# Handing out the operations around each passage between attention and gated units in listed orders

## The chip, the cores and the metric

The kernel runs on one core of a Trainium2 chip. The metric is the device time of one execution in microseconds (us); lower is better. A core has five engines with one in-order queue each: TensorE (PE, matrix products and transposes), VectorE (DVE), ScalarE (ACT), GpSimd (POOL) and SyncE (SP), which issues most transfers. An instruction starts when it is first in its queue and the semaphores it waits for have come. Matrix products write to PSUM banks; other engines read them from there and so give the banks back.

## The reference

The input is (2, 2048, 256) in float32. A first attention block (compressed, selected and windowed attention, combined by gates) comes first, each part wrapped in a layernorm and a residual. Then come two layers of local attention and gated units, and these are where the change lies:

```python
def _layer(x, wqkv, qs, ksc, wo, lg, lb, w1, b1, w2, b2):
    h = shift_token(x)              # second half of the channels moved on by one token
    q, k, v = jnp.split(h @ wqkv, 3, axis=-1)        # 8 heads of 64
    q = l2norm(q) * qs
    k = l2norm(k) * ksc
    q, k = rotary_xpos(q, k)
    o = local_attention(q, k, v)    # windows of 128, each sees itself and the one before
    x = x + o @ wo
    h = shift_token(x)
    h = (h - mu) / jnp.sqrt(var + 1e-05) * lg + lb
    a, g = jnp.split(h @ w1 + b1, 2, axis=-1)        # 682 each
    return x + (a * jax.nn.gelu(g, approximate=False)) @ w2 + b2
for l in range(2):
    x = _layer(x, ...)
```

## The kernel before

The first attention block is recorded and then given out in a listed order (`FIRST`, `Notes.give_out`); it is the same in both kernels. The two layers of attention and gated units follow. There each operation is put into a list `todo` with a place, a number that stands for nanoseconds on a planned time line; at the end the list is sorted by place and every operation is issued in that order. Since each engine has its own in-order queue, the sorted list fixes the order on every engine.

Attention of a layer works on 32 tiles of 128 tokens (`ORDER`: 16 positions, the two batches alternating), one each 12400. For a tile `n` the operations are, with their engines:

- `turn_input` (PE transposes), `early_half`, `late_half` (ACT copies), `edge` (POOL): the shifted input `h`
- `project` j = 1, 0, 2 for keys, queries and values (PE, into a `pa` bank); `square` (ACT), `times` (DVE, rotary products, frees the bank), `values` (ACT)
- `sums`, `clip` (DVE), `power` (POOL), `add` and `unit` (POOL): the normed, rotated queries and keys; `table` (POOL) and `table_load` (SP) prepare the rotary tables
- `turn` (PE), `keys`, `queries` (ACT copies); `scores` (PE, two `pc` banks for each half of the heads), `tops` (DVE maxima with the mask, which frees these banks), `exps` (ACT), `divide` (DVE)
- `turn_probs` (PE, `pb` banks), `probs` (ACT copies), `weigh` (PE), `sum_first` (ACT) and `sum_both` (DVE), both into `oT`; `project_out` (PE) and `residual` (DVE)

The gated units work on eight groups of four tiles (`GORDER`: groups 0, 4, 1, 5, 2, 6, 3, 7), six chunks each, a chunk every 5170 (`STEP`). For a group `g`:

- `shift`: SP copies `Y[g]` one token on into `sh` with two transfers, one of them over 127 partitions, and for all but the first group of a batch a third one from `kept`; POOL writes a memset and `kept`. `sh` takes one of the two buffers that attention's `oT` uses.
- `moments` 0 to 3 (DVE statistics that read `sh`), `deviations` (POOL), `normed` (DVE), `turned` (PE transposes into a `pc` bank, evacuated by DVE), `second_bias` (POOL)
- `inner` (PE, w1), `gate` (ACT Gelu into `ge`, then DVE into `u`), `back` and `back_rest` (PE, w2), `back_add` (DVE)

In the planned order all `gate` operations stand behind the last `exps` (`max(place, no_gate_until)`), `shift` stands two chunks ahead of its `moments`, and the fetches of the next layer's weights have places of their own: `wqkv` and `wo` at 60000 behind the start of the last tile. A fetch that waits holds up what SP issues behind it: `wo` waits until the last `project_out` of the layer has read the old weights.

Banks of PSUM: two `pa`, two `pb`, four `pc`. In the profile nearly every instruction of the two layers has line 124, where `Engine.op` passes a call on; operations are told apart by the names of their tiles.

Of the kernel before, what the change touches and what calls it, by code (L numbers as in the profile page):

```python
# [74 lines left out]
983 870 990 963 904 931 967 965 966 932 968 969 933 970 934 937 935 984 994 971 991 995 936 992 938 972 993 976  # L75
939 997 973 996 940 998 999 977 1000 974 941 1001 975 943 978 942 1002 979 908 1006 871 1003 1007 980 873 905
1004 872 1008 981 909 1005 982 1009 910 911 1010 912 1011 1012
"""


# [73 lines left out]
def sandwich_kernel(ctx: ExitStack, tc: tile.TileContext, x, Wq, bq, Wk, bk, Wv, bv, Wo, bo, Wg, bg,  # L154
# [759 lines left out]
    todo = []  # L914

    def put(place, f, *args):
        todo.append((place, len(todo), f, args))
# [8 lines left out]
    TILE = 12400  # L926
# [265 lines left out]
    STEP = 5170  # L1192
# [154 lines left out]
    W[0]["wqkv"], W[0]["qks"] = attn_w  # L1347
    put(12000, fetch, 0, "wo")
    put(60000, fetch, 0, "gated")
    begin = 0  # L1350
    for l in range(DEPTH):
        last_tile = begin + (len(ORDER) - 1) * TILE
        attention(l, begin)
        units = last_tile + 28150
        last_chunk = units + (NCH * B * NG - 1) * STEP

        gated_units(l, units, last_tile + 37400, last_chunk + (-20000 if l + 1 < DEPTH else STEP))
        if l + 1 < DEPTH:
            put(last_tile + 60000, fetch, l + 1, "wqkv")
            put(last_tile + 60001, fetch, l + 1, "wo")  # L1360
            put(last_chunk + (GT + 1) * STEP, fetch, l + 1, "gated")
            begin = last_chunk - 20000
    with tc.manual_schedule():
        for place, _, f, args in sorted(todo, key=lambda x: x[:2]):
            f(*args)
# [47 lines left out]
```

## Time and profile before

| | us |
|---|---|
| three runs | 1602.71, 1603.73, 1606.21 |
| median | 1603.73 |
| profiled execution, its own time | 1604.54 |
| span of the profiled execution, first to last instruction | 1602.8 |
| first attention block and start (up to about 250) | 250 |
| attention of layer 0 to the gated units' steady state | 250 to 708 |
| gated units of layer 0 | 708 to 895 |
| attention of layer 1 with both passages | 895 to 1381 |
| gated units of layer 1 | 1381 to 1603 |

The span in 40 equal slices, each digit the busy tenths of a slice, and the tenths of full clock that TensorE was granted:

```profile
PE   7999967999999999799999989999999986999998
DVE  6588685787888888444444257888888884355553
ACT  5236554677677676311111146777776763111110
POOL 7205256766666666211111156666666661033243
PEclk9999989999999999889999999999999998999999
```

Slices 17 and 18 and slices 33 and 34 (counted from 1) are the passages into the gated units, slice 24 the one back. Inside attention and inside the gated units TensorE is busy all the time.

### The profile page before, as it was taken

The numbers are of one execution on the slowest core, as the hardware profiler recorded it, in microseconds if no ns is written. First come the engines' busy times: TensorE is split into PE (matmuls) and PEld (weight loads), VectorE is DVE, ScalarE is ACT, GpSimd is POOL, SyncE is SP. The second block draws the span as 40 slices with busy tenths as digits, with TensorE's granted clock in tenths as the row PEclk, the third lists the DMA queues.
The fourth block names the chain that finished last, engine by engine and source line by source line (L and its number), as shares of the span: only waits on it lengthen the run. The fifth ranks groups of instructions, "written<-read, shape, count | busy, mean of one in ns | idle before, by whom it ended". The sixth has DMA issues, their size and how long they took to land.

```text
span 1602.8 us, 32502 instructions
## 1 busy us (share of the span) xinstructions
PE 1519.0 (95%) x12344; PEld 993.6 (62%) x12344; DVE 1070.5 (67%) x3139; ACT 761.7 (48%) x2213; POOL 735.4 (46%) x906
## 2 busy tenths in 40 slices
PE   7999967999999999799999989999999986999998
PEld 6867743666666666455555556667666664555554
DVE  6588685787888888444444257888888884355553
ACT  5236554677677676311111146777776763111110
POOL 7205256766666666211111156666666661033243
PEclk9999989999999999889999999999999998999999
DMA  6000001100000000020000010000000000001000
GB/s 221 1 1 8 1 17 36 33 8 6 8 5 9 5 9 4 8 69 8 12 18 0 1 59 10 9 4 9 6 7 8 8 4 10 10 24 31 25 24 30
DMA packets 32510, 30.76 MB, mean 19 GB/s; under 512 B 5154, under 2 KB 30692, under 8 KB 32356
## 3 DMA queue, kind: packets, MB, share of 16 engines
q1 hardware_dynamic: 32164, 28.17, 5.8%
q8 instruction: 98, 1.61, 0.4%
q0 software_dynamic: 192, 0.52, 0.2%
q14 instruction: 56, 0.46, 0.1%
HBM read 20.30 MB, written 4.19 MB: 15 GB/s over the span
## 4 chain that ended last, share of the span: by engine, by line
PE 74%; DVE 4%; DMA 2%; POOL 1%; ACT 1%; issue 1%; POOLq 0%; SPq 0%; DVEq 0%; ACTq 0%
PE pa L124 29%; PE pb L124 23%; PE pc L124 22%; DMA sh<-Y 2%; DVE prob L124 2%; DVE rr L124 1%; POOL rr L124 1%; DVE Y L124 1%; ACT prob L124 0%; POOL ss L124 0%; DVE hh L124 0%; DVE st L124 0%; DVE ss L124 0%; ACT L124 0%; ACT ge L124 0%
## 5 line engine op out<-in xcount | busy, mean ns | idle before, releaser
L124 PE MATMUL pa<-wqkv,h 128*128 128x512 f32 x768 | 372.6, 608 | 15.1 <-ACT h L124 11.6
L124 POOL TENSOR_TENSOR rr<-rr 128x256 f32<-128x256 f32 x256 | 179.5, 733 | 311.3 <-DVE rr L124 259.3
L124 ACT ACTIVATE ge<-pa,vb 128x512 f32<-128x512 f32 (+1 forms) x107 | 67.0, 628 | 356.5 <-PE pa L124 320.9
L124 ACT ACTIVATE prob<-prob,off 128x192 f32<-128x192 f32 (+2 forms) x512 | 226.2, 445 | 12.7 <-DVE off L124 12.0
L124 PEld LDWEIGHTS pa<-wqkv,h 128*128 128x128 f32 x768 | 132.2, 192 | 128.4 <-issue 106.5
L124 ACT COPY probT<-pb 128x384 f32<-128x384 f32 (+1 forms) x256 | 119.9, 469 | 143.7 <-PE pb L124 140.7
L124 POOL TENSOR_TENSOR ss<-ss,mhalf 128x16 f32<-128x16 f32 x64 | 188.0, 2937 | 0.1
L124 PE MATMUL pa<-hh,w 128*128 128x512 f32 x368 | 176.2, 608 | 5.3 <-ACT ge L124 5.3
L124 DVE SCALAR_TENSOR_TENSOR u<-pb,vb,ge 128x512 f32<-128x512 f32 x73 | 54.8, 751 | 179.8 <-PE pb L124 179.4
L124 DVE CUSTOM_DVE_ANT_0 prob<-pc,mask_loc 128x192 f32<-128x192 f32 (+2 forms) x512 | 148.7, 346 | 28.8 <-PE pc L124 27.5
L124 PE MATMUL pc<-w,u 128*128 128x256 f32 (+1 forms) x896 | 165.3, 383 | 0.0
L124 PEld LDWEIGHTS pc<-w,u 128*128 128x128 f32 (+1 forms) x896 | 129.3, 173 | 50.6 <-issue 35.7
L124 DVE TENSOR_TENSOR rr<-pa,cs 128x1024 f32<-128x1024 f32 x128 | 150.7, 1216 | 10.8 <-ACT sq L124 10.8
L124 PE MATMUL pb<-hh,w 128*128 128x512 f32 x292 | 138.6, 597 | 0.0
L124 POOL TENSOR_TENSOR rr<-rr,ss 128x512 f32<-128x512 f32 x128 | 132.9, 1058 | 2.4
L124 DVE TENSOR_TENSOR prob<-prob,den 128x768 f32<-128x768 f32 x128 | 128.5, 1004 | 4.9
L124 PEld LDWEIGHTS pb<-ident,prob 128*128 128x128 f32 x752 | 89.8, 142 | 66.1 <-DVE prob L124 27.3
L124 PE MATMUL pb<-ident,prob 128*128 128x128 f32 x752 | 118.9, 280 | 11.4 <-DVE prob L124 9.6
L124 PE MATMUL pb<-wo,oT 128*128 128x256 f32 x512 | 123.2, 384 | 5.7 <-DVE oT L124 5.7
L124 POOL TENSOR_SCALAR r<-mv 128x1 f32<-128x1 f32 (+1 forms) x48 | 9.2, 193 | 247.8 <-DVE mv L124 245.4
L124 ACT ACTIVATE sq<-pa 128x512 f32<-128x512 f32 x128 | 75.9, 593 | 96.6 <-PE pa L124 93.8
L124 PE MATMUL pc<-kr,qT 64*64 64x192 f32 (+2 forms) x2688 | 111.0, 289 | 4.5 <-ACT qT L124 4.5
(255 smaller groups left out, 2500.8 us busy)
## 6 DMA issues: line engine op xcount, KB each, us to landing
cs<-in_rope_dram SPq DMA_DIRECT2D x32, 128.0 KB
out_dram<-res SPq DMA_DIRECT2D x32, 128.0 KB
sh<-Y SPq DMA_DIRECT2D x16, 254.0 KB
w<-in_L_ffn_w_dram SPq DMA_DIRECT2D x6, 640.0 KB
X<-_attn_hidden_states_dram SPq DMA_DIRECT2D x7, 512.0 KB
wqkv<-in_L_ffn_wqkv_dram SPq DMA_DIRECT2D x2, 1536.0 KB
Wc<-in_L_attn_Wc_dram SPq DMA_DIRECT2D x1, 1024.0 KB
wo<-in_L_ffn_wo_dram SPq DMA_DIRECT2D x2, 512.0 KB
```

The costliest lines, as they stand in the source:

```text
L124: return f(*a, **k)
```

## The change

The places stay as they are, and so do all operations. After the list is complete, three stretches of it are taken out: around the passage from attention into the gated units in each layer (300 operations, from two and a half tiles before the start of the last tile to nine chunks after the start of the gated units; the same list `TO_GATED` for both layers), and around the passage from layer 0's gated units into layer 1's attention (203 operations, `TO_ATTENTION`). In each stretch the operations, fetches of weights excepted, are given the sorted places again in the listed order: the operation with number `order[k]` gets the k-th place. Fetches keep their places, and so stand at the same rank among other operations than before. The lists were searched offline over a model of in-order queues; the model is not part of the kernel.

```diff
+TO_GATED = """
+39 42 140 0 1 21 26 3 25 28 2 89 9 22 11 17 31 37 19 24 5 8 58 18 20 34 7 12 15 29 41 47 14 4 45 60 27 6 36 48
...
+TO_ATTENTION = """
+45 47 125 128 78 5 18 9 25 10 12 2 6 8 26 33 28 16 17 11 13 30 38 14 37 36 39 7 63 67 19 29 42 43 23 52 70 15 75
...
-    begin = 0
+    begin, seams = 0, []
     for l in range(DEPTH):
         last_tile = begin + (len(ORDER) - 1) * TILE
...
         gated_units(l, units, last_tile + 37400, last_chunk + (-20000 if l + 1 < DEPTH else STEP))
+        seams.append((last_tile - 2.5 * TILE, units + 9 * STEP, TO_GATED))
         if l + 1 < DEPTH:
+            seams.append((last_chunk - 5 * STEP, last_chunk - 20000 + 5 * TILE, TO_ATTENTION))
...
+    def in_order(lo, hi, order):
+
+        part = sorted((x for x in todo if lo <= x[0] < hi and x[2] is not fetch), key=lambda x: x[:2])
+        order = [int(i) for i in order.split()]
+        assert sorted(order) == list(range(len(part)))
+        for x in part:
+            todo.remove(x)
+        todo.extend(part[k][:2] + part[i][2:] for k, i in enumerate(order))
+
+
+    for lo, hi, order in seams:
+        in_order(lo, hi, order)
```

Around the first three groups' `shift` and the first chunks the new order of `TO_GATED` reads, layer 0, with the rank in the stretch (`l0n29` is tile 29 of layer 0, `l0g4` group 4; the bank kinds stand behind `inner`):

```
 100 unit l0n29 0            206 inner l0g0 0 pa pc      281 sum_both l0n31
 101 turn l0n29 0            207 gate l0g0 0             282 project_out l0n31
 102 queries l0n29           208 queries l0n31           283 back l0g0 2
 103 shift l0g0              209 scores l0n31 1          284 residual l0n31
 104 moments l0g0 0          210 scores l0n31 0          285 back l0g0 1
 105 moments l0g0 2          ...                         286 gate l0g4 2
 106 moments l0g0 1          218 inner l0g0 5 pa pb      287 fetch 1 wqkv
 107 moments l0g0 3          219 gate l0g0 5             288 fetch 1 wo
 108 deviations l0g0         220 shift l0g4              289 shift l0g1
 109 exps l0n28 3            221 moments l0g4 0          290 moments l0g1 0
```

In the order before, the ranks are `shift l0g0` 49 and its first `moments` 88; `shift l0g4` 178 and 210; `shift l0g1` 265 and 279, ahead of both fetches (287, 288); the first `gate` 245, the last `exps` 244.

The gelu and the exp are in different function tables of ACT, which it loads with an instruction of its own.

## The prediction

> **What bounds the kernel now.** I read the page's busy shares first, then the stretches, then TensorE (PE) in order of time. PE is busy 95% of the span, so the time is PE's work plus what PE loses. The three stretches below are the three passages that the change touches; the columns are wall time, then busy PE, PEld, DVE, ACT, POOL, then granted clock, DMA share, GB/s.
>
> ```profile
> PE 1519.0 (95%) x12344; PEld 993.6 (62%) x12344; DVE 1070.5 (67%) x3139; ACT 761.7 (48%) x2213; POOL 735.4 (46%) x906
> 636.77:708.17 71.40, 55.33 (x435) 34.51 (x434) 34.45 (x97) 23.95 (x67) 15.81 (x14) 0.86 0.13 40
> 894.94:963.00 68.06, 62.52 (x330) 36.38 (x327) 29.93 (x73) 24.26 (x72) 31.07 (x42) 0.97 0.13 38
> 1312.18:1381.02 68.84, 51.94 (x435) 32.16 (x434) 34.51 (x97) 23.94 (x67) 15.81 (x14) 0.90 0.04 9
> ```
>
> First and third are attention into gated units (layers 0 and 1), the second is the way back. PE idles 16.1, 5.5 and 16.9 us there and then runs at half clock for a while. In full-clock steps of the PE timeline (1.72 us for four 128x512 matmuls, 1.75 for eight `wo`, 1.46 for a `weigh`, 0.8 for a `scores`, 0.49 and 0.35 for four and three transposes) a passage into gated units holds 14x1.72 + 4x1.75 + 3x1.46 + 3x0.8 + 6x0.49 + 11x0.35 = 44.7 us. So layer 0 loses 71.4 - 44.7 = 26.7 us, layer 1 68.8 - 44.7 = 24.1; the way back loses 5.5 idle and 3.3 us at half clock, 7.2. These 58.0 us are all that any order can win.
>
> The chain of waits, the DMA issues (SPq is SyncE's queue) and ACT show two things that an order must respect:
>
> ```profile
> 640.80 0.05 issue
> 640.85 0.20 POOL sh L124
> ...
> 641.65 16.04 DMA sh<-Y
> ...
> 1317.05 16.04 DMA sh<-Y
> ```
> ```profile
> 702.78 0.38 SPq L124 DMA_DIRECT2D wo<-in_L_ffn_wo_dram  x1
> 703.27 0.55 SPq L124 DMA_DIRECT2D sh<-kept  x1
> 703.88 1.46 SPq L124 DMA_DIRECT2D sh<-Y  x2
> ...
> 719.00:720.00 1.00, 1.00 (x5) 0.69 (x4) 0.37 (x1) 0.00 (x0) 0.00 (x0) 1.00 0.08 19
> 720.00:721.00 1.00, 1.00 (x6) 0.89 (x5) 1.00 (x4) 0.00 (x0) 0.29 (x1) 1.00 0.01 2
> ```
> ```profile
> 676.63 0.19 ACT L124 ACTIVATION_READ_ACCUMULATOR prob<-prob,off 128x1 f32 x1
> 676.82 1.28 ACT L124 ACT_TABLE_LOAD   x1
> 678.12 1.27 ACT L124 ACTIVATE ge<-pa,vb 128x512 f32<-128x512 f32 x2
> ```
>
> The transfer of `shift` (`sh<-Y`, 254 KB) lands 16.8 us after its issue (640.86 to 657.70), at 19 GB/s, in both layers; behind the `wo` load it ends 17.6 us after the matmul at 702.6 that let `wo` go. And ACT pays 1.28 us whenever it goes from exp to Gelu.
>
> **The change, part by part.** No instruction's shape changes; only queue positions do. I follow the changed order queue by queue, each operation priced by its row: `times` 1.13, `tops` 1.25, `divide` 1.0, a `moments` 0.64, `normed` 0.26, `u` 0.75 (DVE); Gelu 0.69, copy 0.47 to 0.59 (ACT); `power` 2.94, `unit` 1.06, deviations 1.2 (POOL). Before, `moments` stands far behind its `shift` (first group: issue 589.8, use 618.2). In the new order every moved `shift` is followed at once by its `moments`, on DVE, where all later work queues behind the wait. `shift` moves later past POOL's `add` and `unit`; its own memset and `kept` (0.2 and 0.3) hide there, and POOL has 54% free. SyncE needs only the `sh` buffer.
>
> A, first group, both layers. The buffer comes free with `project_out` of tile 26 (call its end 0), so the data lands at 16.9. DVE still has `residual` and two `tops` and stands at `moments` from 4.6. PE has a `turn`, two `scores`, three `turn_probs`, `turn_input`, two `project`, `weigh`, two `turn` and another `turn_input`, 0.5 + 1.6 + 1.05 + 0.2 + 3.4 + 1.5 + 1.0 + 0.2 = 9.5, and 1.7 in which it waits for ACT's copies of keys and inputs: 11.2 us. Then project 2 of tile 30 needs a `pa` bank that `times` frees, behind `moments`: 16.9 + 2.4 + 1.13 = 20.5. PE idles 20.5 - 11.2 = 9.3 us, twice. Second group: the buffer is free early enough that data and DVE arrive together (39.4 and 39.3 us on the same count): 0, and up to 7 if POOL's place set the issue, which the trace denies (issue 589.8, memset 606.6).
>
> B, table loads and banks, both layers. Gelu now stands among the exps: seven table loads per passage for one, 12 more in all, 12x1.28 = 15.4 us of ACT, of which PE feels what stands in front of it. Running the queues on from A: `queries` of tile 31 behind a Gelu with its load, 1.28 + 0.69 + 0.6 = 2.6 us; `inner` 1 wants a `pc` bank held by the last `scores` until Gelu, `u` and `tops` of the chunk before, 0.69 + 0.75 + 1.25 less a `turn_probs` = 2.5; `weigh` of tile 30 behind four exps and two loads, 1.0; a `turn_probs` behind `u` and `divide`, 1.9; `back` behind two evacuations and the last `u`, 1.8. Sum 9.8. It is soft: none of it if ACT (48% busy) runs ahead, twice it if each load is felt; I take 9.8, since the loads stand directly before what PE waits for.
>
> C, third group (`l0g1`). In layer 0 the fetches of `wqkv` and `wo` keep their places while `shift` moves behind them on SyncE's queue, so it is issued only when `wo` goes, after tile 31's `project_out`: exactly the three DMA rows above, 17.6 us. Then 2.4 for `moments`, 1.2, six `normed` 1.6, `u` 0.75, `back_add` 0.35: 23.9. PE has two `back`, one `inner`, one `back` and its rest, 2.2 + 3.4 + 1.1 + 0.6 = 7.3, then transposes that need `normed`. Idle 16.6 us. In layer 1 no fetch stands there; the issue comes after tile 30's `project_out`, 12.1 us of PE work earlier (three `inner` and a `project_out`), and idle is 16.6 - 12.1 = 4.5, less 0.5 without `wo`'s data in front: 4.0, bounds 0 and 7. The fourth group's transfer queues behind the third's: 0 to 2, taken as 0.
>
> D, the way back has no `shift`, no extra table load and the same fetches. The new order puts `project`, `inner` and `back` between transposes and `scores`, which covers the 2.25 us wait at 923.8 and the 0.5 to 0.7 us ones; remaining 2 us of 7.2, bounds 0 and 7.2.
>
> Clock. The rows show PE at 0.50 for 3.3 us after a wait of 2.2 us or more (659.9 to 663.0, 680.4 to 683.7), 1.65 us lost, 3.4 where a second wait follows. Four such waits per passage: 6.6 each. The Trainium skill (TensorE: Matmul & The Clock Gate, part 1) gives the window as 3.4 us and free-running, which these rows agree with; by its word that one idle window is needed, the two waits of 2.5 us in B might cost nothing, 3.3 us less per passage.
>
> Sum: layer 0 loses 9.3 + 9.8 + 16.6 + 6.6 = 42.3, layer 1 9.3 + 9.8 + 4.0 + 6.6 = 29.7, the way back 2: 74.0 for 58.0, +16. The profiled execution took 1604.5 us (span 1602.8 and 1.7 around it), the median of the runs is 1603.7: 1603.7 + 16 = 1620.
>
> One rule speaks against the order outright: the Trainium skill (DMA: Bandwidth & Descriptors, "Rules for kernel authors") says to issue early and wait late. The same page ("Why a DMA increments its semaphore by 16 and not by 1") says that a transfer over 127 partitions uses one DMA engine; the rows' 0.08 share, 1.3 of 16 engines, agrees. From its 27 GiB/s per engine and 2 us fixed, an estimate of the landing is 11 us instead of 16.8; by it A would be 3.5 us, C 10.8 and 0, and the time 1598. The trace's 16.8 decides.
> On table loads the skill (ScalarE: Activation LUTs, "What ACT_TABLE_LOAD costs") adds 1.38 us of drain to each; the rows above show none (load ends 678.10, Gelu starts 678.12). With it ACT would lose 16.6 us more.
>
> **Rivals.**
> Faster: the queues run ahead and B vanishes, the layer-1 transfer of C is covered and the way back is clean. For it: DVE, ACT and POOL have 33 to 54% free. Losses 9.3 + 16.6 + 3.3 and 9.3 + 1.7, 40.2 in all, 1604 - 18 = 1586. It decides once B is under some 5 us a passage. Against: the loads are in the order, and ACT is one queue.
> About even: A and C as I have them, B halved with two restarts fewer per passage: 16 - 9.8 - 6.6 = -0.4, 1603.
> Much slower: every table load is felt and restarts cost 3.4 each: B 19.6 per passage, so 2x9.8 + 8x1.75 = 33.6 on my sum, 1654; half of that, 1637, is as far as I go.
> That the change does nothing is out: the orders differ on all five queues in the three passages.
>
> **Numbers.** Forecast (A and C stand, B between half and one and a half times) 0.66; much slower 0.12; about even 0.08; faster 0.14. This kernel's measurement can tell 0.2%, 3.2 us. Of the forecast's 0.66 nearly all lies over 1606.9: slower 0.79, same 0.07, faster 0.14. Time 1620; range 1600 to 1637, from just below even to half of the worst B.
>
> **What would show it.** In the new profile: the chain of waits passes through `DMA sh<-Y` at three places in layer 0; DVE's wait for `DMA sh<-Y` rises from 2.0 us to some 35 in sum over both layers; PE has a wait near 9 us before a `wqkv` matmul in each layer and one near 16 before the transposes of `hh` in layer 0; 15 table loads instead of 3; the way back at full clock. I am wrong if `shift` lands well under 16 us after its issue, or if DVE comes to `moments` late.

## The result and the profile after

The changed kernel takes 1628.09 us (median of four runs, 1626.39 to 1628.78) against 1604.20 before (1602.71 to 1606.21): a ratio of 1.0146, 95% interval 1.0134 to 1.0158. The profiled execution took 1627.85 us with a span of 1626.1, so 23.3 us of span were added to 1602.8.

The page of the changed kernel: busy time, share and number of instructions of an engine, then the tenths of the clock that TensorE was granted, then the chain that ended last.

```profile
PE 1518.6 (93%) x12344; PEld 989.9 (61%) x12344; DVE 1064.0 (65%) x3139; ACT 773.9 (48%) x2225; POOL 736.3 (45%) x906
PEclk9999979999999998998999999999999989999999
PE 70%; DVE 4%; DMA 4%; ACT 3%; POOL 2%; issue 1%; SPq 0%; POOLq 0%; DVEq 0%; ACTq 0%
```

PE's busy time is that of before (1519.0) to 0.4 us, although the span is 23.3 us longer. So PE was given no more work; it waits longer. ACT has 12 instructions more (2213 before), the table loads, and 12.2 us more (761.7 before).

What PE waits for, and what DVE waits for (sum, number of waits, longest):

```profile
PE pa L147 <- DVE rr L147: 19.3, 5, 9.2
PE pc L147 <- DVE Y L147: 15.4, 3, 13.9
PE pb L147 <- DVE prob L147: 11.8, 6, 2.8
...
PE pb L147 <- ACT probT L147: 7.3, 6, 3.1
PE pc L147 <- ACT probT L147: 5.7, 4, 2.6
```
```profile
DVE st L147 <- DMA sh<-Y: 42.7, 6, 16.8
```

Before, DVE waited 2.0 us in sum for `sh<-Y`, now 42.7. The two largest waits of PE are for DVE: DVE is the one that stands still, and PE only inherits it. The same in order of time on PE in layer 0; in brackets stands the idle time ahead of the instruction and who ended it.

```profile
635.82 3.78 PE L147 MATMUL pa<-wqkv,h 128*128 128x512 f32 x4 [9.17 <-DVE rr L147]
...
648.45 0.84 PE L147 MATMUL pb<-ident,prob 128*128 128x128 f32 x6 [2.64 <-DVE prob L147]
...
678.62 0.55 PE L147 MATMUL pb<-ident,prob 128*128 128x128 f32 x3 [3.10 <-ACT probT L147]
...
693.59 0.56 PE L147 MATMUL pc<-probT,v 64*64 64x128 f32 x16 [2.63 <-ACT probT L147]
...
697.46 1.54 PE L147 MATMUL pb<-ident,prob 128*128 128x128 f32 x6 [2.80 <-DVE prob L147]
...
722.65 4.48 PE L147 MATMUL pc<-w,u 128*128 128x256 f32 x20
...
730.40 3.35 PE L147 MATMUL pc<-w,u 128*128 128x256 f32 x26
747.62 1.12 PE L147 MATMUL pc<-ident,hh 128*128 128x128 f32 x4 [13.87 <-DVE Y L147]
```

The chain of waits names what stands behind the first and the last of these:

```profile
616.15 16.12 DMA sh<-Y
635.82 3.78 PE pa L147 x4
...
724.74 16.20 DMA sh<-Y
748.74 3.41 PE pa L147 x4
```

In layer 1 the same five waits of the first group and of the exponentials are there (9.01, 2.60, 3.09, 2.63 and 2.77 us), and the last one is 1.30 us, where layer 0 has 13.87.

Where the 23.3 us came from is read off one event that both traces have, POOL's copy `kept` of a group. The eighth `kept` (the last group of layer 0) starts at 829.73 before and at 851.36 after, 21.6 later, of which 0.7 us was there before the change begins (POOL's `power` at 589.62 before stands at 590.27 after). The last one of all starts at 1507.63 and 1530.96, 23.3 later. In between, the way back takes 61.06 us where it took 68.06 (894.94 to 963.00 before):

```profile
916.58:977.64 61.06, 59.89 (x322) 33.56 (x321) 32.18 (x81) 25.49 (x74) 31.87 (x38) 1.00 0.14 43
```

So layer 0's passage costs 21.0 us more, the way back wins 7.0, and layer 1's passage costs 8.7 more: +0.7 + 21.0 - 7.0 + 8.7 = +23.4 (23.3 before rounding). The offset wanders by some 0.3 us inside layer 1's attention, so the parts are known no better than that.

### The profile page after: what moved, and what is told of

The parts are those of the page before. It is cut to its first block, busy times and chain, and to the rows that moved or that the text cites. A ratio compares the mean times of both kernels' runs of the same rounds, so it can differ in the third digit from the quotient of the medians.

```text
span 1626.1 us, 32484 instructions
## 1 busy us (share of the span) xinstructions
PE 1518.6 (93%) x12344; PEld 989.9 (61%) x12344; DVE 1064.0 (65%) x3139; ACT 773.9 (48%) x2225; POOL 736.3 (45%) x906
## 4 chain that ended last, share of the span: by engine, by line
PE 70%; DVE 4%; DMA 4%; ACT 3%; POOL 2%; issue 1%; SPq 0%; POOLq 0%; DVEq 0%; ACTq 0%
PE pa L147 27%; PE pb L147 23%; PE pc L147 20%; DMA sh<-Y 4%; ACT L147 1%; DVE hh L147 1%; DVE prob L147 1%; POOL rr L147 1%; ACT prob L147 1%; DVE rr L147 1%; DVE u L147 1%; POOL ss L147 1%; DVE Y L147 1%; ACT ge L147 0%; DVE st L147 0%
## 5 line engine op out<-in xcount | busy, mean ns | idle before, releaser
L147 PE MATMUL pb<-ident,prob 128*128 128x128 f32 x752 | 118.3, 280 | 18.5 <-DVE prob L147 11.8
L147 DVE TENSOR_TENSOR prob<-prob,den 128x768 f32<-128x768 f32 x128 | 124.9, 976 | 4.9
```

The source lines that it names most:

```text
L147: return f(*a, **k)
```

## The experiments

All are built on the changed kernel unless it says before. Each batch of runs has its own runs of the kernel before beside it (median 1603.92 to 1604.97).

| run | what is different | us | ratio to before, 95% |
|---|---|---|---|
| changed kernel | | 1628.09 | 1.0146 (1.0134 to 1.0158) |
| back_only | only the list of the way back | 1597.74 | 0.9958 (0.9941 to 0.9975) |
| third_first | `shift l0g1` ahead of the fetches | 1614.36 | 1.0062 (1.0045 to 1.0079) |
| wait_later | first group's `moments` later on DVE | 1615.87 | 1.0066 (1.0046 to 1.0087) |
| split | transfer cut into 112 + 15 partitions | 1589.94 | 0.9902 (0.9886 to 0.9919) |
| split_prime | transfer cut into 113 + 14 partitions | 1623.07 | 1.0120 (1.0103 to 1.0137) |
| grouped | 3 table loads per passage in place of 7 | 1611.03 | 1.0041 (1.0027 to 1.0056) |
| split_grouped | both | 1570.88 | 0.9791 (0.9775 to 0.9808) |
| split_identity | split, Gelu replaced by the identity: no table loads in the layers | 1568.63 | 0.9779 (0.9763 to 0.9795) |
| before_split | before, with the transfer cut | 1600.47 | 0.9969 (0.9956 to 0.9982) |
| back_split | back_only, with the transfer cut | 1590.71 | 0.9915 (0.9898 to 0.9931) |

**The way back alone.**

```diff
-    for lo, hi, order in seams:
+    for lo, hi, order in seams[1:2]:
```

> Only the list for the way back is given out; both passages into the gated units keep the order before. My account: the changed kernel's offsets say that this list saves 7.0 us, so 1597 (1595 to 1599) against 1604. Rival, that the way back gained only because the passage in front of it came out differently: 1604, as before.

Measured: 1597.74 us. From 1604.94 beside it that is -7.2 us, what the trace of the changed kernel gives for the way back inside the whole (-7.0). So the way back's gain does not hang on the passages, and the two passages into the gated units cost 1628.1 - 1597.7 = 30.4 us.

**The third group's shift ahead of the fetches** (265 is `shift l0g1`, 247 `project_out` of tile 30; both layers):

```diff
+        if order[0] == 39:
+            order.remove(265)
+            order.insert(order.index(247) + 1, 265)
```

> The changed kernel, with shift of the third group given out right behind tile 30's project_out, ahead of the fetches of wqkv and wo. My account (step C: the transfer queues behind wo, which waits for the last project_out): the 13.9 us wait of PE in layer 0 shrinks to some 1.5 us, the restart goes with it, 1628 - 12.5 - 2 = 1613 (1611 to 1616); layer 1 unchanged. Rival, that DVE is late there for its own work: 1628.

Measured: 1614.36 us, 13.7 less. In order of time on PE, the wait before the transposes of `hh`:

```profile
735.86 0.66 PE L147 MATMUL pc<-ident,hh 128*128 128x128 f32 x4 [2.14 <-DVE Y L147]
```

13.87 us have become 2.14. Of the 13.7 us, 11.7 are this wait; what is left of the gain fits the half clock that followed it (0.55 from 748 to 753 in the changed kernel, 2.3 us lost). So it was the place behind the fetches on SP's queue that made layer 0's third group late.

**The first group's statistics later on DVE** (88 and 95 to 110 are the four `moments` and the `deviations` of `l0g0`, 143 is its first `normed`):

```diff
+        if order[0] == 39:
+            late = [order.pop(order.index(88)) for _ in range(1)] + [order.pop(order.index(i)) for i in (100, 95, 105, 110)]
+            order[order.index(143) : order.index(143)] = late
```

> The changed kernel, with the first group's four moments given out behind times, sum_both and sums of the next tile, shift where it is. My account (step A: what is queued behind the wait on DVE costs, not the transfer itself): the 9.2 and 9.0 us waits of PE before project 2 of tile 30 go, at most 2 us of each come back, 1628 - 16 - 3 = 1609 (1606 to 1615). Rival, that the wait only moves to the next bank on the path: 1625 or more.

Measured: 1615.87 us, 12.2 less, and just outside of what was expected. PE's wait of 9.17 us is gone, but in its place stands, a little later:

```profile
638.58 1.51 PE L147 MATMUL pb<-ident,prob 128*128 128x128 f32 x6 [5.87 <-DVE prob L147]
```

DVE still comes to the `moments` before the data, but now by 2.04 us instead of 10.01, and what queues behind them is a `divide` instead of a `times`. Ahead of that `divide` DVE also runs the `moments` themselves and waits 1.43 us for POOL's `deviations`. So this edit handed a shorter wait to another victim; whether some other place would have taken it out of the way was not tried.

**The transfer cut in two.** The trace says that the large transfer of a `shift` (127 partitions) runs at 19 GB/s with a DMA share of 0.08, 1.3 of 16 engines. Cutting it at 112 partitions changes nothing else but the number of issues:

```diff
-            nc.sync.dma_start(sh[1:P, :, :], y[0 : P - 1, :, P:H])
+            nc.sync.dma_start(sh[1:113, :, :], y[0:112, :, P:H])
+            nc.sync.dma_start(sh[113:P, :, :], y[112 : P - 1, :, P:H])
```

> The changed kernel in its order, with the transfer over 127 partitions cut into one over 112 and one over 15, so that it can spread over more DMA engines. My account (A and C are the 16 to 18 us from issue to landing): landing some 4 us after issue, both waits before project 2 gone, the third group's wait down from 13.9 to about 3, 1628 - 18 - 11 - 5 for restarts = 1594 (1588 to 1600). Rival 1, that the rate is set by the 512-byte pieces and not by the partition count: landing and time unchanged, 1628. Rival 2, that the order of the banks costs without the transfer: 1610 or more.

Measured: 1589.94 us, 38.2 us less than the changed kernel and 1% less than before. Stretches of the changed kernel and then of this one around the first `shift` (wall time, then busy PE, PEld, DVE, ACT, POOL, then granted clock, DMA share, GB/s); the issue is at 615 to 616 in both:

```profile
618.00:620.00 2.00, 1.76 (x12) 1.24 (x12) 1.21 (x9) 1.30 (x4) 1.92 (x5) 1.00 0.06 14
620.00:622.00 2.00, 2.00 (x6) 0.80 (x6) 1.97 (x10) 0.23 (x1) 1.92 (x4) 1.00 0.10 29
622.00:630.00 8.00, 4.41 (x78) 2.87 (x76) 0.35 (x2) 4.52 (x14) 0.13 (x1) 0.98 0.08 19
```
```profile
618.00:620.00 2.00, 1.76 (x24) 1.10 (x16) 0.54 (x3) 0.86 (x2) 1.92 (x4) 1.00 0.53 130
620.00:622.00 2.00, 2.00 (x8) 1.13 (x8) 1.97 (x12) 0.43 (x2) 1.92 (x3) 1.00 0.03 8
622.00:630.00 8.00, 7.76 (x101) 4.45 (x100) 6.31 (x21) 4.68 (x15) 4.25 (x9) 1.00 0.00 1
```

The data is there some 4 us after the issue instead of 16, in one burst with a mean DMA share of 0.53. From 622 to 630 DVE works 6.31 us where it worked 0.35. The waits of 9.17 and 2.64 us are gone; the longest that stand in that part now are 0.97 us before a `weigh` and 1.16 before a `scores`. The 13.87 becomes 1.32. The waits of 3.10 and 2.63 us for the exponentials' side stay as they were and the 2.80 is 2.47, so they have next to nothing to do with the landing.

**Cut at another place.** Is it the cut that helps, or the count of partitions?

```diff
-            nc.sync.dma_start(sh[1:P, :, :], y[0 : P - 1, :, P:H])
+            nc.sync.dma_start(sh[1:114, :, :], y[0:113, :, P:H])
+            nc.sync.dma_start(sh[114:P, :, :], y[113 : P - 1, :, P:H])
```

> The changed kernel with the shift's transfer cut in two at another place: 113 and 14 partitions (both runs that cut it into 112 and 15 landed in about 4 us). Theory (the count of partitions decides over how many DMA engines a transfer is spread; 113 is a prime like 127, so this piece stays on one engine): the large piece lands about 16.1 x 113/127 = 14.3 us after its issue, the waits of 9.17 and 13.87 us fall by less than 2 us each, and the time is about 1622 us (1616 to 1627). Rival (two transfers in place of one are what helps, by being smaller or by running beside each other): as with 112 and 15, 1588 to 1596 us.

Measured: 1623.07 us. One partition more in the large piece takes away nearly the whole gain. The chain of waits of this run:

```profile
617.65 14.06 DMA sh<-Y
```

14.06 us against 16.12 for 127 partitions is 0.87, and 113/127 is 0.89: the time goes with the number of partitions, as it would if one engine carried them all, and the DMA share stays at 0.09 from 622 to 630. PE's waits of 9.17 and 13.87 us are 7.98 and 12.79. The rival, that two smaller transfers are quicker as such, is out.

**Grouping the table loads.** 213 and 215 are the `exps` of tile 30 for the first two pairs of heads, which stood between Gelus; 199 is the one for the third pair, given out before them; 246 and 264 are two `gate` of the first group:

```diff
+        if order[0] == 39:
+            for i, j in ((213, 199), (215, 213)):
+                order.remove(i)
+                order.insert(order.index(j) + 1, i)
+            order.remove(246)
+            order.insert(order.index(264), 246)
```

ScalarE in the changed kernel, around the wait of 2.63 us that ends at 693.59 (start, duration):

```profile
688.02 1.28 ACT L147 ACT_TABLE_LOAD   x1
689.32 0.69 ACT L147 ACTIVATE ge<-pa,vb 128x512 f32<-128x512 f32 x1
690.02 1.28 ACT L147 ACT_TABLE_LOAD   x1
691.32 0.45 ACT L147 ACTIVATE prob<-prob,off 128x192 f32<-128x192 f32 x1
...
693.08 0.46 ACT L147 COPY probT<-pb 128x384 f32<-128x384 f32 x1
693.56 1.28 ACT L147 ACT_TABLE_LOAD   x1
694.85 0.69 ACT L147 ACTIVATE ge<-pa,vb 128x512 f32<-128x512 f32 x1
```

A single Gelu of 0.69 us between exponentials brings two loads of 1.28 us; the copy that PE's `weigh` waits for stands behind both, and the next Gelu, whose result DVE needs ahead of a `divide`, behind a third.

The split kernel without any table change (this is what leaves the Gelu out), and with the loads grouped:

> The changed kernel with the shift's transfer cut in two (112 and 15 partitions), and with the Gelu of the gated units replaced by the identity, so that ScalarE has no table to change inside the layers; the order of the work is that of the changed kernel. Theory (the waits of 2.5 to 3.1 us that are left in the two passages come from the table loads between the exponentials and the Gelus, and each lowers the clock behind it): the three of them in each passage, 3.10 + 2.63 + 2.47 = 8.2 us, go, with some 2 to 4 us of half clock; 1589.9 - 2 x (8.2 + 3) = about 1568 us (1562 to 1575), and the trace shows no wait over 1.5 us on turn_probs or weigh. Rival (the banks of PSUM and the order of the copies hold TensorE, and the loads only lie beside it): the waits stay and the time is 1587 to 1591 us.

> The changed kernel with the transfer cut in two, and in both passages the two exponentials of tile 30 that stood between Gelus moved up behind the exponentials of the same tile that come before them, and one Gelu of the first group moved down to stand with the next: 3 table loads per passage in place of 7, the whole computation. Theory (loads are what TensorE waits for): of the three waits of 2.5 to 3.1 us in each passage two go, with the half clock behind them: 1589.9 - 2 x (5.3 + 1 to 3) = about 1576 us (1572 to 1582). Rival (the order of the copies and banks, not the loads): within 3 us of 1589.9.

> The changed kernel with only the grouping of the table loads (3 per passage in place of 7), the transfer whole. With the cut transfer the grouping took 1589.9 to 1570.9, 19.0 us. If landings and loads are independent: 1628.1 - 19 = about 1609 us (1605 to 1613), with the waits of 9.2 and about 13.9 us still there. Rival (part of the loads' time is hidden under the late landing, or the reverse): 1613 to 1622 us.

Measured: split_identity 1568.63, split_grouped 1570.88, both against 1589.94 for split; grouped 1611.03 against 1628.09. split_grouped came out 1 us under the range expected of it. The rival (banks and order of the copies) is out for two of the three waits: in split_identity the 2.63 and the 2.47 are gone, in split_grouped the 2.63 is gone and the 2.47 is 1.58. The page of split_grouped, and PE in order of time:

```profile
PE 1504.6 (96%) x12344; PEld 983.5 (63%) x12344; DVE 1065.0 (68%) x3139; ACT 762.4 (49%) x2217; POOL 737.9 (47%) x906
...
PEclk9999988999999999999999999999999999999999
```
```profile
663.23 0.55 PE L147 MATMUL pb<-ident,prob 128*128 128x128 f32 x3 [1.82 <-ACT probT L147]
...
677.97 0.87 PE L147 MATMUL pb<-ident,prob 128*128 128x128 f32 x6 [1.58 <-DVE prob L147]
...
713.50 0.66 PE L147 MATMUL pc<-ident,hh 128*128 128x128 f32 x4 [1.12 <-DVE Y L147]
```

No wait is over 2 us in the passages of either layer, and the granted clock is 1.00 in both (620 to 720 and 1270 to 1370 us). That is where the rest of the gain is: PE's busy time fell by 14.0 us from the changed kernel's 1518.6 with the same 12344 matmuls, and half clock in the passages cost the changed kernel 14.3 us (counted below), which is gone here. One part of the theory failed. The wait of 1.82 us at `turn_probs` is there in split_identity too (the expectation said none over 1.5): of the 3.10 us, only 1.3 went with the loads; in split_identity the copies that `turn_probs` waits for still stand on ACT behind the last chunk's two activations, the second of which waits for DVE. And split_identity is only 2.3 us under split_grouped, with ranges that overlap (1568.20 to 1571.38 and 1569.82 to 1572.16) and with another order of the `exps` and `gate`: the loads that are left cost little, and how little is not resolved.

Loads and landings are nearly independent: grouping alone takes 17.1 us, and 19.0 once the transfer is quick.

**The cut transfer under the order of before**, with and without the list of the way back (the same edit of the transfer, in the kernel before and in back_only):

> The kernel before with nothing but the shift's transfer cut in two. Theory (the 127-partition transfer costs the kernel before as well, where its oT waits 2.23 and 3.49 us for the shifted half and where the fetches of the query weights lie behind it on SP's queue): these waits and the restart behind each go in both passages, 1604.9 - 8 = about 1597 us (1593 to 1601). Rival (there the transfer is covered, and its waits are taken by the next thing that is late): 1603 to 1606 us.

> The kernel before with the searched order on the way back to attention alone, and with the shift's transfer cut in two. If the gains are independent: 1597.7 - 8 = about 1590 us (1586 to 1594), as much as the whole searched order gives with the cut transfer (1589.9): then the searched orders of the two passages into the gated units are worth nothing even with a transfer that lands early. Rival (the searched order of the passages is better than the former one once the landing is early): over 1594 us here.

Measured: 1600.47 and 1590.71, -4.5 and -7.0 us. The gain came out smaller than the 8 us in the kernel before, and its waits did not go: PE's wait for `oT` fell from 5.7 us in sum (longest 3.5) to 3.4 (longest 1.7), so `oT` is late for another reason too, which was not followed further. With back_split, the question of what the searched passages are worth is answered in steps. With the slow transfer they cost 30.4 us (1628.1 against 1597.7). With the quick one they are worth nothing (1589.9 against 1590.7). With the loads grouped as well they win 19.8 us (1570.9 against 1590.7). The version with both edits takes 2.1% less than the kernel before (95% interval 1.9 to 2.3%) and 3.5% less than the changed one (1570.88 / 1628.09).

## Why the prediction was right, and where it was off

The direction and the mechanism were right: 1620 forecast with a range from 1600 to 1637, 1628 measured. The terms, in us of TensorE time lost per passage:

| term | forecast, layer 0 / 1 | measured, layer 0 / 1 |
|---|---|---|
| A, first group | 9.3 / 9.3 | 9.17 / 9.01 |
| B, loads and banks | 9.8 / 9.8 | 13.2 / 13.1 |
| C, third group | 16.6 / 4.0 | 13.87 / 1.30 |
| clock restarts | 6.6 / 6.6 | 8.26 / 6.05 |
| sum | 42.3 / 29.7 | 44.5 / 29.5 |
| loss of before | 26.7 / 24.1 | 25.1 / 22.5 |
| added by the change | 15.6 / 5.6 | 19.4 / 7.0 |
| way back, what remains of 7.2 | 2 | 1.2 |

A and C are the waits on PE, and B is all other idle time from 603 to 765 and from 1292 to 1430 us. The clock's row is PE's busy time in each microsecond times what the granted clock lacked of 1.00; the loss of before is its idle time (16.1 and 16.9) and the same count of its clock (9.1 and 5.6). The offsets above say 21.0 and 8.7 where this count says 19.4 and 7.0: 1.6 and 1.7 us are in no row.

- **A was right to 0.3 us**, and for the reason given: DVE stands at `moments`, and the `pa` bank that `times` has to free comes late. wait_later and split both moved it. What the forecast left out is the second wait behind the same cause: 2.64 us (2.60 in layer 1) at 648.45 for a `divide` that queues on DVE behind the late work. It went with the cut transfer and stayed with the grouped loads (2.74), so it belongs to A and not, as this table's division has it, to the loads. With it A costs 11.8 and 11.6.
- **B was the term that came out largest against its forecast, +3.4 and +3.3, and not in its places.** Without the wait that belongs to A it is 10.6 and 10.5, near 9.8. The 2.6 us at `queries` came out as 0.20, and the 2.5 us for a `pc` bank did not come. What came are 3.10 us at a `turn_probs`, 2.63 at a `weigh` and 2.80 at a `turn_probs`, 8.5 in sum. That loads stand in front of these waits holds for most of the 8.5 us (grouped, split_identity); the number was luck, a sum of wrong parts.
- **C was too large by 2.7 us in both layers, and one price did most of it**: a `back` was counted as 1.1 us and the rest of it as 0.6, both at half. A `back` is ten matmuls, 2.15 us; the row of 20 above (4.48 us) is two of them, and the profile of before has ten in 2.32 us. PE's cover ahead of the transposes was therefore 733.75 - 722.65 = 11.1 us instead of 7.3. The chain itself, from the matmul that releases `wo` to the transposes, was 747.62 - 722.65 = 25.0 where 23.9 was worked out. That the fetches set the issue was right (third_first).
- **The clock came out near, partly by luck**: 13.2 us forecast, 14.3 measured. The forecast counted four waits over 2.2 us per passage with a restart of 1.65 us each, and two of its four were waits that did not come. Measured are six such waits in layer 0 and five in layer 1, but only four and three stretches of half clock, each worth some 2 us of work. In layer 0 (wall time, then busy PE, PEld, DVE, ACT, POOL, then granted clock, DMA share, GB/s):

```profile
637.00:640.00 3.00, 3.00 (x12) 0.92 (x14) 2.97 (x6) 0.36 (x1) 2.88 (x5) 0.52 0.00 0
650.00:653.00 3.00, 3.00 (x66) 2.88 (x59) 2.25 (x11) 1.82 (x8) 0.00 (x0) 0.52 0.02 5
680.00:683.00 3.00, 3.00 (x11) 1.48 (x10) 1.91 (x9) 0.70 (x2) 0.00 (x0) 1.00 0.62 226
695.00:698.00 3.00, 0.54 (x3) 0.55 (x4) 2.39 (x5) 1.39 (x3) 0.00 (x0) 0.50 0.01 3
698.00:700.00 2.00, 2.00 (x7) 1.47 (x6) 0.60 (x3) 0.96 (x2) 1.19 (x2) 0.50 0.00 0
748.00:753.00 5.00, 5.00 (x10) 2.41 (x9) 2.58 (x5) 0.69 (x1) 0.78 (x1) 0.55 0.08 19
```

  Half clock follows the waits of 9.17, 2.64 and 13.87 us. It also follows the 2.63, from 694.5 on, and the 2.80 behind it falls into the same stretch. After the 3.10 the clock stays at 1.00, while in layer 1 the 3.09 is followed by half clock (1367 to 1370) and the 2.60 is not. The Trainium skill (TensorE: Matmul & The Clock Gate, part 1) says that the clock falls after an idle window of about 3.4 us. All these waits of 2.6 to 3.1 us are shorter, and four of the eight lowered the clock all the same, so here its rule did not save the short ones.
- **Where the miss comes from.** The span grew by 23.3 us where 16 were forecast. The terms behind the change, taken together, were short by only 1.2 us (2.0 in the passages, less 0.8 on the way back), because B came out 6.7 us larger and C 5.4 smaller, which is luck too. Another 3.2 us lie in the loss of before: the count of full-clock steps gave 50.8 us for the two passages, and idle time and half clock add up to 47.6. The remaining 2.9 us are not placed; 0.7 of them stand ahead of the change.
- **The way back** was better than forecast by 0.8 us: 1.2 us of idle time are left in it, no wait over 0.67, at full clock.
- **The landing**: 16.0 to 16.2 us on the chain, as in the profile of before. DVE's wait for it is 42.7 us in sum where some 35 were forecast, and the chain passes through it at two places in layer 0 and not at three: the second group's landing is not on it. The estimate of 11 us from the skill's rate was wrong in size, but its rule for the number of engines (DMA: Bandwidth & Descriptors, "Why a DMA increments its semaphore by 16 and not by 1") is what split and split_prime show: 112 partitions are carried by many engines (share 0.53), 127 and 113 are not (0.08 and 0.09).
- **The rivals.** Faster and about even needed B under 5 us or halved; its three waits alone make 8.5. Much slower needed B at 19.6 and restarts of 3.4 us; B is 13.2 and 13.1, and a restart costs some 2.

That the searched lists lose because their model had a short landing and free table loads is only argued: the model isn't in the kernel. Shown is that with the landing short and three operations of `TO_GATED` moved, so that there are fewer loads, the lists win.

## What to carry to other kernels

An instruction that waits for a transfer costs what queues behind it on its in-order engine, so price a moved wait by the next bank or buffer which that engine has to free, and price the transfer by its measured landing. Before reordering around a slow transfer, look at its DMA share: here 112 + 15 partitions in place of 127 took 38 us off the changed order, and 4.5 us off the order of before, where DVE waited only 2.0 us for the landing. And count the waits over about 2 us, not only their sum, since TensorE's half clock behind some of them made up 14 of the 74 us lost in the two passages.

## What was not expected of the hardware

- A transfer between two tiles in SBUF of 112 partitions and 224 KB landed in about 4 us, one of 113 partitions took 14 us; 15 and 112 partitions together took a quarter of the time of 127.
- What SP issues right behind a slow transfer is held up too: the issue of `wqkv` occupies SP's queue 11.74 us in the changed kernel (11.73 before) and 0.55 us in split; the issue of a `kept` transfer right behind the third group's takes 11.81 us in the changed kernel and 0.61 in split.
- The three longest waits left in layer 0's passage of split_grouped, 1.82, 1.58 and 1.16 us, left the granted clock at 1.00; of the changed kernel's eight waits of 2.6 to 3.1 us four lowered it, two fell into half clock that was there already, and two left it at 1.00.
- Eight table loads fewer, 8 x 1.28 = 10.2 us on ACT, gave 17 to 19 us. From split to split_grouped PE's idle time in the two passages falls by some 10 us, and 7.5 us of half clock go with it.
